# Roots by ln and exp, sums by TensorE, and a split first LayerNorm in a two-layer MetaFormer

## The chip, the core and the metric

The kernel runs on one core of a Trainium2 chip, in float32. The metric is the device time of one execution in microseconds (us). A separately profiled execution gives the trace. The core's engines are TensorE (PE in the profile, its weight loads PEld), VectorE (DVE), ScalarE (ACT), GpSimd (POOL) and SyncE (SP). Each works through its own instructions in order; semaphores tie them together. Data moves by 16 DMA engines, whose transfers are issued from an engine's queue.

## The reference

The input x is (4, 384, 32, 32): four batches, 384 channels, 1024 positions. Two layers, each a mixer and a feed-forward part, with residuals:

```python
# layer 0
x = x + selective_scan_block(layernorm_c(x))
t = tokens(x)
t = t + experts(layernorm(t))
# layer 1
x = x + attention(layernorm_c(x))
t = tokens(x)
out = t + kron_ffn(layernorm(t))
```

The selective scan reads the positions in four directions. For each direction it projects x to 12 + 16 + 16 rows, forms dt by a softplus, and runs `h = h*exp(dt*A) + dt*u*B`, `y = sum_n h*C` over 1024 steps with 16 states per channel. The four directions are added, normalized over channels, scaled, and put through an exact GELU. The feed-forward part of layer 0 chooses two of four experts per token (384 to 1536 to 384, GELU) and adds their outputs weighted by the two gates. Attention has eight heads of 64 with one matrix for queries, keys and values. In the last feed-forward part both matrices are Kronecker products (32 by 12 factors): each token's 384 channels are first multiplied by a vector `c2` of 12 repeated numbers and summed in groups of 12, which leaves 32 numbers per token, called z here.

## The kernel before

The program has two strands. `scan_layer` does layer 0's mixer for batches 0 to 3, one after the other, in 32 units (batch, direction, half of 512 positions). `tail_batch` does everything else of a batch: `route`, `experts`, `combine`, `prologue`, `attention` and `last_layers`. Batch b's tail is woven into the scan of batch b+1 and after; the last batch's routing, experts, attention and last layers stand behind the scan alone, together with what is left of batch 2's. A planner in the framework puts the instructions of both strands in one order per engine; `high_priority` marks those to be put forward (combine, prologue, last layers, and a part of the routing). On the chip the order is fixed.

**The scan.** `start(b)` (L219) loads x of a batch in one transfer and normalizes both halves with `layernorm` (L149). TensorE makes the channel mean by a product with ones (`ln_mean`, L157), DVE subtracts it (L159), ScalarE squares (L166), TensorE sums the squares (`ln_var`, L172), ScalarE takes the root (L178), DVE the reciprocal (L180), TensorE spreads it over the partitions (`ln_rows`, L183) and DVE multiplies (L188). `project` (L289) makes a unit's projections (`xd_ps`, L318), dt by softplus, and writes rows to DRAM, from which they are read back spread over the partitions (`dtr<-dd`, `bcs<-rows`). Chunk by chunk, POOL multiplies dt*u by B (`bx`, L420), ScalarE takes the exponential (`da`, L429), DVE scans (L434), DVE and POOL multiply by C (L441, L448), and TensorE accumulates (`acc`, L455). `finish(b)` (L225) normalizes the sum y, applies Gelu (ScalarE, L228), adds x (POOL, L236) and writes x1 to DRAM. Then the next batch's scan follows.

**ScalarE's tables.** A root needs another activation table than Exp, and Gelu another again. `exp_again` (L141) loads the table with exp and ln back after each root and each Gelu. The instruction is ACT_TABLE_LOAD in the profile: L144 is this reload, and a load on the line of a root is the load for that root.

**The tail.** `route` transposes a batch to tokens, computes gate scores and token statistics, finds for each token its two experts' places, and (L649 to L654, in `spread`) normalizes each block of 128 tokens on DVE and scatters it by POOL's indirect DMA to both places. `experts` runs 11 slots of 256 or 128 rows; weights come by SP. A slot ends with `y_ps` (TensorE, L895), the bias (DVE, L899) and a transfer of y to `made` in DRAM (L900, SP's queue). `combine` (L904) gathers for each token block both experts' rows from `made` (POOL, L913), multiplies each by its gate into PSUM (ScalarE, L920) and adds both to the tokens `xt` (DVE, L924). `prologue` (L930) takes token statistics (`stats`, L516, with a root at L525 and a reciprocal), normalizes (DVE, L531) and transposes to `xc` (`tc_ps`, TensorE, L939). `attention` (L946) begins with products on `xc` (`w_ps`, L964). `last_layers` (L1047) adds the output bias (POOL, L1077), forms the output projection in pairs of token blocks (`o_ps`, L1083, added at L1087), takes the statistics, multiplies all of xt by c2 (`prod`, L1091), sums in groups of 12 (`zt`, L1093), corrects for mean and root (L1098 to L1102), and goes on with `z_ps` (L1108), the hidden products and the output.

**Buffers.** The tail's room has, while the scan runs, 8 buffers `kw` (128x768), 2 of `k12` (128x3072), 5 of `k4` (128x1024), and one pair of PSUM banks that `two` hands out for `w_ps` of combine, `tc_ps`, `s_ps`, `o_ps`, `z_ps` and `h_ps`; for batch 3's attention and last layers there are two such pairs.

Of the kernel before, what the change touches and what calls it, by code (L numbers as in the profile page):

```python
# [12 lines left out]
ALU = mybir.AluOpType  # L13
# [101 lines left out]
class Body:  # L115
    def __init__(self, ctx, tc, a):
        self.tc, self.nc, self.a = tc, tc.nc, a
        nc = self.nc
        const = ctx.enter_context(tc.tile_pool(name="const", bufs=1))
        self.const = const  # L120

        self.cols = const.tile([P, NCOL], F32, tag="cols", name="cols")
        nc.scalar.dma_start(out=self.cols, in_=a["cols"])

        self.ident = const.tile([P, P], F32, tag="ident", name="ident")
        make_identity(nc, self.ident)
        self.ones = const.tile([P, P], F32, tag="ones", name="ones")
        nc.gpsimd.memset(self.ones, 1.0)
        self.eps5 = const.tile([P, 1], F32, tag="eps5", name="eps5")
        nc.gpsimd.memset(self.eps5, 1e-5)  # L130
        self.eps6 = const.tile([P, 1], F32, tag="eps6", name="eps6")
        nc.gpsimd.memset(self.eps6, 1e-6)

        self.minus1 = const.tile([P, 1], F32, tag="minus1", name="minus1")
        nc.gpsimd.memset(self.minus1, -1.0)

        self.c2sum = const.tile([P, 1], F32, tag="c2sum", name="c2sum")
        lo, hi = COL["c2"]
        nc.vector.tensor_reduce(self.c2sum, self.cols[:, lo:hi], AX.X, ALU.add)
# [5 lines left out]

    def col(self, name, i):
        at = COL[name][0] + i
        return self.cols[:, at : at + 1]

    def layernorm(self, src, dst, eps, psum, work):  # L150

        nc = self.nc
        for i in range(NH):
# [16 lines left out]
            for m in range(nm):  # L170
# [6 lines left out]
            self.exp_again(  # L177
                nc.scalar.activation(std, var[:, :nm], AF.Sqrt, bias=eps, scale=1.0 / D).ins  # L178
            )
            nc.vector.reciprocal(std, std)  # L180
# [11 lines left out]
    def scan_layer(self, x1, between):  # L192

        nc, tc, a = self.nc, self.tc, self.a
        with ExitStack() as ctx:
# [23 lines left out]
            def start(b):  # L219
                x = work.tile([P, DC, L], F32, tag="u", name="u")  # L220
                nc.sync.dma_start(out=x, in_=a["x"][b].rearrange("(c p) l -> p c l", p=P))
                self.layernorm(x, x, self.eps6, psum, work)
                return x
# [26 lines left out]
            for _ in self.project(units[0], us[0], wx, work, dram, psum, ahead):  # L250
                pass
            self.under_way = {}
# [232 lines left out]
    def first_layer(self, b, room):  # L485

        self.experts(b, self.slots, room)
        with self.tc.high_priority(offset=FORWARD):
            xt = self.combine(b, *self.place, room)
            return self.prologue(xt, xt, room)  # L490
# [25 lines left out]
    def stats(self, xt, eps, room):  # L516
# [8 lines left out]
        self.exp_again(nc.scalar.activation(rstd, mv[:, :, 1], AF.Sqrt, bias=eps).ins)  # L525
        nc.vector.reciprocal(rstd, rstd)
        return mv[:, :, 0], rstd

    def normalize(self, xt, mean, rstd, out):
        for m in range(MB):  # L530
            self.nc.vector.tensor_scalar(  # L531
                out[:, m, :], xt[:, m, :], mean[:, m : m + 1], rstd[:, m : m + 1],
                op0=ALU.subtract, op1=ALU.mult,
            )
# [71 lines left out]
    def spread(self, b, x1, room):  # L606
# [29 lines left out]
        self.exp_again(nc.scalar.activation(rstd, mv[:, :, 1], AF.Sqrt, bias=self.eps5).ins)  # L636
        nc.vector.reciprocal(rstd, rstd)
        nc.vector.tensor_mul(sc, sc, rstd.unsqueeze(2).to_broadcast([P, MB, NE]))
        nc.vector.tensor_add(sc, sc, self.bg.unsqueeze(1).to_broadcast([P, MB, NE]))
        pos, gate, expert = self.places(sc, room)  # L640
# [4 lines left out]
        for m in range(MB):  # L645
            if m % 2 == 0:
                xt = room.tile([P, 2, D], "k4", "xt")
                nc.sync.dma_start(out=xt, in_=self.tokens(b)[:, m : m + 2, :])
            nc.vector.tensor_scalar(  # L649
                xt[:, m % 2, :], xt[:, m % 2, :], mv[:, m, :1], rstd[:, m : m + 1],  # L650
                op0=ALU.subtract, op1=ALU.mult,
# [155 lines left out]
    def experts(self, b, routed, room):  # L807
# [57 lines left out]
        for s in range(NSLOT):  # L865
# [34 lines left out]
            nc.sync.dma_start(  # L900
# [3 lines left out]
    def combine(self, b, pos, gate, room):  # L904

        nc = self.nc
        xt = room.tile([P, MB, D], "k12", "xt")
        nc.sync.dma_start(out=xt, in_=self.tokens(b))
        got = []
# [7 lines left out]
        for m in range(MB):  # L917
            ps = room.two("w_ps")
            for k in range(TOP):
                nc.scalar.activation(  # L920
                    ps[:, k, :D], got[m][:, k, :], AF.Copy, scale=gate[:, k, m : m + 1]
                )
            for k in range(TOP):
                nc.vector.tensor_add(xt[:, m, :], xt[:, m, :], ps[:, k, :D])  # L924
        nc.sync.dma_start(out=self.tokens(b), in_=xt)
        return xt
# [3 lines left out]
    def prologue(self, xt, xn, room):  # L930

        nc = self.nc
        mean, rstd = self.stats(xt, self.eps6, room)
        self.normalize(xt, mean, rstd, xn)
        xc = room.tile([P, DC, L], "k12", "xc")
        for c in range(DC):
            ps = room.two("tc_ps")
            for m in range(MB):
                nc.tensor.transpose(  # L939
                    ps[:, m // 4, m % 4 * P : (m % 4 + 1) * P], xn[:, m, c * P : (c + 1) * P],  # L940
# [108 lines left out]
    def last_layers(self, b, att, room):  # L1049
# [27 lines left out]
        nc.gpsimd.tensor_add(xt, xt, bout.unsqueeze(1).to_broadcast([P, MB, D]))  # L1077
        for m in range(0, MB, 2):
# [8 lines left out]
            nc.vector.tensor_add(xt[:, m : m + 2, :], xt[:, m : m + 2, :], ps[:, :, :D])  # L1087

        mean, rstd = self.stats(xt, self.eps5, room)
        prod = room.tile([P, MB, D], "k12", "prod")  # L1090
        nc.vector.tensor_mul(prod, xt, c2.unsqueeze(1).to_broadcast([P, MB, D]))  # L1091
        zt = room.tile([P, MB, KR], "zt", "zt")
        nc.vector.tensor_reduce(  # L1093
            zt.rearrange("p m r -> p (m r)"), prod.rearrange("p m (r j) -> p (m r) j", j=KJ),
            AX.X, ALU.add,
        )
# [61 lines left out]
    def second_layer_exact(self):  # L1158

        nc, tc, a = self.nc, self.tc, self.a  # L1160
        with ExitStack() as ctx:
# [10 lines left out]
            for b in range(B):  # L1172
                xc = work.tile([P, DC, L], F32, tag="xc", name="xc", bufs=1)
                att = work.tile([P, HEADS // 2, L], F32, tag="att", name="att", bufs=1)
                with ExitStack() as part:
# [4 lines left out]
                    nc.vector.tensor_copy(xc, self.prologue(xt, xt, room))  # L1180
# [205 lines left out]
```

## Time and profile before

| | |
|---|---|
| median of 3 runs | 4482.44 us (4480.09 to 4482.89) |
| profiled execution | 4517.48 us, span 4513.6 us |
| granted TensorE clock | 0.831 |
| TensorE, VectorE, ScalarE, GpSimd busy | 76, 67, 56, 67% of the span |
| activation table loads | 92 of the exp table again (118.0 us), 28 before a root (35.9 us) |
| experts' products times gates (ScalarE, L920) | 64, 37.3 us |
| adding them (VectorE, L924) | 64, 35.3 us |
| normalizing in the prologue (VectorE, L531) | 32, 23.0 us |
| normalizing in the routing (VectorE, L649) | 32, 30.4 us |
| product with c2 and its sums (VectorE, L1091, L1093) | 4 and 4, 17.3 and 13.3 us |

Each row is a group of instructions of one line and engine: how many there are in the whole execution, and how long they were busy together. The profiled execution takes longer than the timed ones; sums of instruction times are to be held against its own time. In the lines below, `out<-in` names the tiles, sizes are partitions by elements, "xN" counts the instructions; after the bar stand busy time and the mean of one in ns, then the engine's idle time just before them and what ended it. In an ordered listing the first two numbers are start and length in us, and a bracket gives the idle time before it, with its releaser. A line of a stage has its start and end, its length, then the busy time of each engine with the number of instructions, the granted clock, the DMA engines' busy share and GB/s.

### The profile page before, as it was taken

To read this page: it belongs to the slowest core of one execution; us is meant where nothing else is said; L and a number is where in the kernel's file an instruction comes from. 1 tells how busy PE (TensorE), PEld (TensorE's weight loads), DVE (VectorE), ACT (ScalarE), POOL (GpSimd) and SP (SyncE) were. 2 spreads that over 40 slices of the span, in tenths; PEclk is the share of its full clock that TensorE was granted. 3 is DMA by queue.
4 is the path that set the end of the run, shared out by engine and by line. 5 is a ranking of instruction groups with operands and counts; after the bars stand their busy time and mean duration, and the time that the engine had idled before them with its cause. 6 is when DMAs were issued, how large, how long until landed. Compare 5 with 4: busy or idle time off the path is not lost. (4 is left out here: it accounts for less than half of the span.)

```text
span 4513.6 us, 46925 instructions
## 1 busy us (share of the span) xinstructions
PE 3440.6 (76%) x13852; PEld 1652.0 (37%) x13852; DVE 3010.8 (67%) x4344; ACT 2534.3 (56%) x4406; POOL 3037.0 (67%) x1467
## 2 busy tenths in 40 slices
PE   6545554479894787669998588757998689999796
PEld 2111121145552222225555222214555445556333
DVE  4999997878878977977877777896778520002102
ACT  4555554456665676466666577556666444334554
POOL 4999998788987877778988778878889510000100
PEclk7666665589996898669998699858999789999897
DMA  4444554477886533457779443445787543344200
GB/s 119 118 123 118 146 136 106 137 230 209 231 240 181 149 84 104 130 159 226 210 220 275 137 114 101 115 139 170 232 244 232 169 157 115 107 127 153 75 16 15
DMA packets 404361, 684.81 MB, mean 152 GB/s; under 512 B 50944, under 2 KB 206464, under 8 KB 404096
## 3 DMA queue, kind: packets, MB, share of 16 engines
q1 hardware_dynamic: 395360, 656.16, 50.3%
q0 software_dynamic: 8192, 25.17, 1.7%
q8 instruction: 111, 1.82, 0.2%
q14 instruction: 154, 1.26, 0.1%
q10 hardware_dynamic: 544, 0.40, 0.0%
HBM read 561.47 MB, written 120.06 MB: 151 GB/s over the span
## 5 line engine op out<-in xcount | busy, mean ns | idle before, releaser
L420 POOL TENSOR_TENSOR bx<-dtr,bcs 128x1024 f32<-128x1024 f32 x768 | 1797.8, 2366 | 227.7 <-PE acc L455 103.5
L429 ACT ACTIVATE da<-dtr,nega 128x512 f32<-128x512 f32 x1536 | 1045.5, 691 | 1039.4 <-DVE bx L441 569.0
L448 POOL TENSOR_TENSOR bx<-bx,bcs 128x1024 f32<-128x1024 f32 x384 | 903.6, 2358 | 211.8 <-DVE bx L434 88.0
L455 PE MATMUL acc<-bx,sel 128*32 128x512 f32 x3072 | 511.8, 713 | 312.4 <-POOL bx L448 248.8
L879 PE MATMUL h_ps<-xc,w 128*128 128x256 f32 (+1 forms) x3168 | 680.1, 370 | 61.7 <-DVE xc L861 31.5
L895 PE MATMUL y_ps<-w,hs 128*128 128x384 f32 x1824 | 649.9, 509 | 49.8 <-ACT hs L888 44.1
L879 PEld LDWEIGHTS h_ps<-xc,w 128*128 128x128 f32 x3168 | 557.2, 200 | 253.4 <-issue 120.4
L434 DVE TENSOR_TENSOR_SCAN bx<-da,carry,bx 128x512 f32<-128x512 f32 x384 | 474.0, 1269 | 118.6 <-POOL bx L420 65.5
L434 DVE TENSOR_TENSOR_SCAN bx<-da,bx 128x512 f32<-128x512 f32 x384 | 452.2, 1209 | 129.2 <-POOL bx L420 70.3
L434 DVE TENSOR_TENSOR_SCAN da<-da,carry,bx 128x512 f32<-128x512 f32 x384 | 476.5, 1273 | 67.9 <-ACT da L429 62.6
L441 DVE TENSOR_TENSOR bx<-da,bcs 128x512 f32<-128x512 f32 x768 | 509.8, 679 | 3.8
L434 DVE TENSOR_TENSOR_SCAN da<-da,bx 128x512 f32<-128x512 f32 x384 | 456.3, 1218 | 60.7 <-ACT da L429 44.2
L895 PEld LDWEIGHTS y_ps<-w,hs 128*128 128x128 f32 x1824 | 352.3, 198 | 341.7 <-issue 86.4
L992 ACT ACTIVATE ex<-s_ps 128x512 f32<-128x512 f32 x512 | 299.4, 591 | 274.9 <-PE s_ps L987 259.9
L987 PE MATMUL s_ps<-w 64*128 64x512 f32 x1024 | 308.4, 674 | 83.1 <-ACT ex L992 74.2
L1077 POOL TENSOR_TENSOR xt<-xt,wb 128x3072 f32<-128x3072 f32 x4 | 26.8, 6708 | 477.5 <-DMA w<-in_w 345.5
L1036 PE MATMUL o_acc<-ex,vt 128*64 128x512 f32 x1024 | 295.6, 658 | 0.8 <-ACT att L1044 0.8
L455 PEld LDWEIGHTS acc<-bx,sel 128*32 128x32 f32 x3072 | 77.7, 117 | 596.0 <-POOL bx L448 363.8
L884 ACT ACTIVATE hs<-h_ps,bb 128x256 f32<-128x256 f32 (+1 forms) x528 | 194.0, 447 | 128.8 <-PE h_ps L879 128.5
L899 DVE TENSOR_TENSOR y<-y_ps,bb 128x384 f32<-128x384 f32 x76 | 41.6, 548 | 237.6 <-PE y_ps L895 237.6
L913 POOL DMA_INDIRECT got<-made,g_pos x64 | 60.8, 950 | 192.4 <-PE f_acc L1136 159.1
L987 PEld LDWEIGHTS s_ps<-w 64*128 64x128 f32 x1024 | 81.1, 192 | 266.8 <-ACT ex L992 149.1
(216 smaller groups left out, 4021.9 us busy)
## 6 DMA issues: line engine op xcount, KB each, us to landing
w<-in_w SPq DMA_DIRECT2D x352, 576.0 KB
dtr<-dd SPq DMA_DIRECT2D x1536, 128.0 KB
bcs<-rows SPq DMA_DIRECT2D x512, 128.0 KB
dd<-one_e SPq DMA_DIRECT2D x96, 256.0 KB
dd<-mag SPq DMA_DIRECT2D x96, 256.0 KB
rows<-zero SPq DMA_DIRECT2D x76, 192.0 KB
xs<-rows SPq DMA_DIRECT2D x32, 384.0 KB
made<-y SPq DMA_DIRECT2D x32, 384.0 KB
```

The source lines that it names most:

```text
L420: pool = nc.gpsimd.tensor_mul(bx, dtr[q][1], bc[:, 0].unsqueeze(1).to_broadcast([P, 2, HF])).ins
L429: nc.scalar.activation(da, dtr[q][0][:, j, :], AF.Exp, scale=nega[:, col : col + 1])
L434: nc.vector.tensor_tensor_scan(run(h), run(da), run(bx[:, j, :]), 0.0 if first else hold, ALU.mult, ALU.add,)
L441: dve = nc.vector.tensor_mul(bx[:, j, :], h, cg).ins
L448: pool = nc.gpsimd.tensor_mul(bx, bx, cg.unsqueeze(1).to_broadcast([P, 2, HF])).ins
L455: nc.tensor.matmul(acc[lo : lo + DB, :], sel, out[q][:, j, :], start=(g == 0), stop=(g == NG - 1),)
L879: nc.tensor.matmul(ps[:, r, :], w1[(f + r) // wf][:, c, (f + r) % wf * P : ((f + r) % wf + 1) * P], xc[:, c, :], start=(c == 0), stop=(c = ...
L884: nc.scalar.activation(hs[:, f + r, :], ps[:, r, :], AF.Identity, bias=bb[:, f + r : f + r + 1])
L895: nc.tensor.matmul(out[:, :D], hs[:, f, t * P : (t + 1) * P], w2[f // wf][:, f % wf, :], start=(f == 0), stop=(f == FC - 1),)
L987: nc.tensor.matmul(ps[:, o, :], w[rows, j * P : (j + 1) * P], w[rows, halves(i)], start=True, stop=True,)
L992: ins = nc.scalar.activation(ex[:, o, :], ps[:, o, :], AF.Exp, scale=HD**-0.5, accum_out=sums[:, t, 2 * j + o, i : i + 1],).ins
L1036: ins = nc.tensor.matmul(out[cols, :], made[t][1][:, j, cols], ex[:, o, :], start=(j == 0), stop=(j == MB - 1),).ins
```

## The change

1. The table with exp and ln is loaded as ScalarE's first instruction of all.
2. A root's reciprocal is made by two activations of that table, `exp(-0.5 * ln(var + eps))`, in `layernorm` (16 sites), `stats` (8) and the routing (4). The root, both table loads and the reciprocal on DVE go.
3. Normalizing in the routing and in the prologue moves from DVE to ScalarE: Identity with scale = rstd and bias = -mean*rstd, the latter made by one small DVE instruction. The prologue's result goes into the gathered buffers `got`, no longer into `xt`.
4. `combine`: POOL makes, for both experts, eight diagonal 128x128 tiles of the gates; TensorE multiplies them with the gathered rows and adds both experts in PSUM; DVE adds a pair of blocks at once.
5. The last expert slot's `made` transfer is issued from ScalarE's queue instead of SP's.
6. `last_layers`: the product with c2 and its sums are made for each pair of blocks behind its output projection; the product goes to the same PSUM bank.
7. The first batch's x is loaded in two halves. Only its first half is normalized before the first unit's projections, the second half behind them.

```diff
+        nc.scalar.preload_act_table_set("natural_log_exp_and_others")
         self.cols = const.tile([P, NCOL], F32, tag="cols", name="cols")
...
+    def inverse_root(self, out, var, eps, scale=1.0):
+        self.nc.scalar.activation(out, var, AF.Ln, bias=eps, scale=scale)
+        self.nc.scalar.activation(out, out, AF.Exp, scale=-0.5)
...
-    def layernorm(self, src, dst, eps, psum, work):
+    def layernorm(self, src, dst, eps, psum, work, parts=range(NH)):
-        for i in range(NH):
+        for i in parts:
...
-            self.exp_again(
-                nc.scalar.activation(std, var[:, :nm], AF.Sqrt, bias=eps, scale=1.0 / D).ins
-            )
-            nc.vector.reciprocal(std, std)
+            self.inverse_root(std, var[:, :nm], eps, scale=1.0 / D)
...
-                nc.sync.dma_start(out=x, in_=a["x"][b].rearrange("(c p) l -> p c l", p=P))
-                self.layernorm(x, x, self.eps6, psum, work)
+                src = a["x"][b].rearrange("(c p) l -> p c l", p=P)
+                if b > 0:
+                    nc.sync.dma_start(out=x, in_=src)
+                    self.layernorm(x, x, self.eps6, psum, work)
+                    return x
+                for i in range(NH):
+                    nc.sync.dma_start(out=x[:, :, halves(i)], in_=src[:, :, halves(i)])
+                self.layernorm(x, x, self.eps6, psum, work, parts=[0])
                 return x
...
             for _ in self.project(units[0], us[0], wx, work, dram, psum, ahead):
                 pass
+            self.layernorm(us[0], us[0], self.eps6, psum, work, parts=range(1, NH))
...
+    def less_mean(self, mean, rstd, room, tag):
+        less = room.tile([P, MB], tag, "less")
+        self.nc.vector.scalar_tensor_tensor(less, mean, -1.0, rstd, op0=ALU.mult, op1=ALU.mult)
+        return less
...
-            nc.vector.tensor_scalar(
-                xt[:, m % 2, :], xt[:, m % 2, :], mv[:, m, :1], rstd[:, m : m + 1],
-                op0=ALU.subtract, op1=ALU.mult,
+            nc.scalar.activation(
+                xt[:, m % 2, :], xt[:, m % 2, :], AF.Identity,
+                bias=less[:, m : m + 1], scale=rstd[:, m : m + 1],
             )
...
-            nc.sync.dma_start(
+            queue = nc.sync if s + 1 < NSLOT else nc.scalar
+            queue.dma_start(
                 out=made[at : at + size, :].rearrange("(t p) d -> p t d", p=P), in_=y
             )
...
+        diag = []
+        for k in range(TOP):
+            d = room.tile([P, MB, P], "k4", "diag")
+            nc.gpsimd.tensor_mul(
+                d, self.ident.unsqueeze(1).to_broadcast([P, MB, P]),
+                gate[:, k, :].unsqueeze(2).to_broadcast([P, MB, P]),
+            )
+            diag.append(d)
...
-        for m in range(MB):
+        for m in range(0, MB, 2):
             ps = room.two("w_ps")
-            for k in range(TOP):
-                nc.scalar.activation(
-                    ps[:, k, :D], got[m][:, k, :], AF.Copy, scale=gate[:, k, m : m + 1]
-                )
-            for k in range(TOP):
-                nc.vector.tensor_add(xt[:, m, :], xt[:, m, :], ps[:, k, :D])
+            for o in range(2):
+                for k in range(TOP):
+                    nc.tensor.matmul(
+                        ps[:, o, :D], diag[k][:, m + o, :], got[m + o][:, k, :],
+                        start=(k == 0), stop=(k == TOP - 1),
+                    )
+            nc.vector.tensor_add(xt[:, m : m + 2, :], xt[:, m : m + 2, :], ps[:, :, :D])
...
-        return xt
+        return xt, [got[m][:, 0, :] for m in range(MB)]
...
         mean, rstd = self.stats(xt, self.eps6, room)
-        self.normalize(xt, mean, rstd, xn)
+        less = self.less_mean(mean, rstd, room, "less")
+        for m in range(MB):
+            nc.scalar.activation(
+                xn[m], xt[:, m, :], AF.Identity, bias=less[:, m : m + 1], scale=rstd[:, m : m + 1]
+            )
...
-            nc.vector.tensor_add(xt[:, m : m + 2, :], xt[:, m : m + 2, :], ps[:, :, :D])
+            pair = xt[:, m : m + 2, :]
+            nc.vector.tensor_add(pair, pair, ps[:, :, :D])
+            nc.vector.tensor_mul(ps[:, :, :D], pair, c2.unsqueeze(1).to_broadcast([P, 2, D]))
+            for o in range(2):
+                nc.vector.tensor_reduce(
+                    zt[:, m + o, :], ps[:, o, :D].rearrange("p (r j) -> p r j", j=KJ),
+                    AX.X, ALU.add,
+                )
...
-        prod = room.tile([P, MB, D], "k12", "prod")
-        nc.vector.tensor_mul(prod, xt, c2.unsqueeze(1).to_broadcast([P, MB, D]))
-        zt = room.tile([P, MB, KR], "zt", "zt")
-        nc.vector.tensor_reduce(
-            zt.rearrange("p m r -> p (m r)"), prod.rearrange("p m (r j) -> p (m r) j", j=KJ),
-            AX.X, ALU.add,
-        )
```

## The prediction

> **What bounds the kernel now.** I read the table of engine busy times first, then the same busy times by stage, then the routing windows, then the order of time at the start and the end.
>
> The page's first part:
>
> ```profile
> PE 3440.6 (76%) x13852; PEld 1652.0 (37%) x13852; DVE 3010.8 (67%) x4344; ACT 2534.3 (56%) x4406; POOL 3037.0 (67%) x1467
> ```
>
> No engine is full over the span, so the bound moves. By stage (start:end in us, length, then busy time of each engine, granted clock, DMA share, GB/s):
>
> ```profile
> 60.00:790.00 730.00, 389.90 (x1194) 114.81 (x1192) 651.59 (x876) 388.11 (x602) 694.11 (x303) 0.66 0.49 125
> ...
> 2690.00:3554.00 864.00, 710.42 (x2963) 350.55 (x2961) 695.10 (x968) 534.76 (x920) 717.78 (x335) 0.88 0.59 174
> 3554.00:3690.00 136.00, 87.77 (x339) 46.73 (x340) 45.63 (x154) 62.41 (x124) 37.97 (x38) 0.72 0.56 187
> 3690.00:4190.00 500.00, 484.65 (x2011) 284.51 (x2007) 46.87 (x81) 192.13 (x388) 7.66 (x2) 0.98 0.37 117
> ```
>
> The first batch's scan, which has no tail work beside it, is POOL's (694 of 730 us), with DVE close behind. In the scans of batches 1 to 3 POOL and DVE are each busy near 80%: POOL is the steady limit and gives way in stretches. From 3690 us TensorE is the bound (485 of 500). So an edit is worth what it gives POOL or DVE before 3554 us, what it takes from a chain in which both wait, and what it gives TensorE after that. The three routing stretches are DVE's:
>
> ```profile
> 840.00:900.00 60.00, 18.83 (x43) 3.57 (x43) 59.64 (x114) 18.59 (x29) 40.63 (x20) 0.51 0.45 124
> 1860.00:1920.00 60.00, 26.31 (x86) 10.05 (x86) 59.93 (x83) 31.15 (x42) 36.79 (x18) 0.50 0.39 112
> 2940.00:3000.00 60.00, 30.64 (x101) 13.67 (x100) 59.59 (x102) 28.13 (x43) 45.38 (x21) 0.53 0.50 144
> ```
>
> DVE is full for 60 us in each, and POOL has 15 to 23 us to spare.
>
> **What the Trainium skill says.** "ScalarE: Activation LUTs", Table sets: the hidden batching unit: exp and ln share natural_log_exp_and_others, sqrt has another set, so exp, sqrt, exp is two switches. Same page, What ACT_TABLE_LOAD costs: about 1283 ns of load, with a drain of about 1380 ns. The trace has 1283 ns for every load; an activation starts 20 ns after its load, so I count the load alone. "SBUF — State Buffer", Who interferes with whom: DVE and GpSimd share a port pair; two-port DVE forms and DVE operations with two SBUF inputs contend with it, ScalarE and TensorE never do. The trace agrees: the same 128x384 subtract-and-multiply takes 465 ns at its fastest and 2542 ns at its slowest in the first routing stretch. "DMA: Bandwidth & Descriptors", Issuing engines are not separate DMA queues: another issuing engine saves only sequencer time, so the moved `made` DMA is worth no bandwidth.
>
> **The change part by part** (negative is faster).
>
> *Start: −12.* Now the second half's LayerNorm stands before the projections:
>
> ```profile
> 8.08 4.47 PE L157 MATMUL ln_mean<-u,ones 128*128 128x512 f32 x6 [8.08 <-DMA u<-in_x]
> ...
> 19.70 1.28 ACT L178 ACT_TABLE_LOAD   x1 [4.56 <-PE ln_var L172]
> ...
> 34.61 4.80 PE L318 MATMUL xd_ps<-u,wx 128*44 128x512 f32 x6
> ```
>
> The second half's rows are made at 32.61 and xd_ps follows 2.0 us later. The first half's rows are made at 21.62; without the table load (1.28) and the reciprocal they come at about 20.3, so xd_ps at 22.3: −12.3. The halved transfer lands sooner: the whole took 7.3 us, so 0 to 3.5 us. Against it, the second half's LayerNorm (TensorE about 9 us, DVE 4) now stands ahead of the first accumulations; the first POOL multiply waits from 35 to 61 us for projections, softplus and two DMAs, which covers most. I give back 4. The early table load itself is worth nothing: the first Exp waits until 3.79 us for the column DMA, after the load has ended at 2.97. Ends: −8 and −16.
>
> *Table loads in the scan's LayerNorms: −10.* 28 roots lose two loads each: 56 × 1.283 = 72 us of ScalarE, which is not the bound. They count where everybody waits: POOL stands before the final x + y of each batch for the Gelu (72.0 us over four batches), and inside that wait lie two root loads: 4 × 2 × 1.28 = −10. The second activation of each root (0.26) replaces the reciprocal (0.17). Ends: −5, and −20 if the exp loads are in it too.
>
> *Routing's normalization off DVE: −20.* In the three full stretches it takes 11.5, 8.2 and 7.3 us of DVE, together 27.0. ScalarE gets 8 × about 0.6 us in each (between the 476 ns of its 128x384 copy and an estimate of 0.69 from the activation price of that page with two pointers), and is busy 19 to 31 of 60 there. I count three quarters, as scatters on POOL follow. Ends: 0 if POOL's chain takes over at once, −27.
>
> *Combine and prologue in the scan, batches 0 and 1: −10.* Per batch DVE loses 16 × 0.551 + 8 × 0.791 = 15.1 and gains 4 × 0.948 = 3.8; ScalarE loses 16 × 0.584 = 9.3 and gains 8 × 0.6. DVE is the limit about half of the time there: half of 11.3 a batch, rounded down. Ends: 0, −22.
>
> *Diagonal tiles on POOL: +14.* Two 128x1024 products per batch. The trace has no such product; POOL's nearest, the same size with a broadcast operand, takes 2.366 us: 4.7 per batch, on the bound for three batches. The fourth pair runs while POOL is idle. Ends: 0 if made in a POOL wait; +20 if contention lengthens them.
>
> *Combining products on TensorE: +5.* 16 × 0.51 us (an expert's 128x384 product) = 8 per batch, beside waits that exist already in the scan, but they stand as one block that waits for the gathers, with later scan products behind it. Ends: 0, +15.
>
> *Last layers per pair: −5.* In the scan DVE exchanges 4.33 + 3.32 for 4 × 0.95 + 8 × about 0.5 (the reduce row's 1.08 ns per element): equal. The held PSUM bank delays the next pair's products by about 2 us, behind which scan products stand ready. At the end it counts: the whole-tile product and reduce after the last o_ps take
>
> ```profile
> 4439.10 3.34 DVE L1091 TENSOR_TENSOR prod<-xt,wb 128x3072 f32<-128x3072 f32 x1
> ...
> 4442.51 3.32 DVE L1093 TENSOR_REDUCE zt<-prod 128x256 f32<-128x3072 f32 x1
> ```
>
> = 6.66; one pair's share, 0.95 + 2 × 0.5, stays: −4.7. Ends: −3, −6.
>
> *Where the work now stands: 0, from −35 to +50.* The largest unknown. Compared in engine order, the tail's POOL work moves 10 to 20 scan products (24 to 47 us) forward: batch 2's 16 gathers stood after the scan's last product and now stand 10 products before it; its attention starts before the last accumulation. Now, 3554 to 3628 us holds 39.7 us of TensorE work, so up to 34 us of idleness could be filled. But the gathers wait for the last expert's `made`, and the gathers themselves took 20 us, in order ahead of 10 products at 2.37. Batch 3's combine gains from the shorter path (the last y_ps ends at 4184.25, attention's first product starts at 4247.19: 63 us now; about 42 worked out of gathers 21, last pair's product and add, statistics, root, normalizing and transposes), but the 31 us of batch 2's last layers that TensorE does inside that gap now stand ahead of it: −21 + 31 = +10, unless they fill earlier idle time. The last `made` DMA moves to ScalarE's queue, where it waits for y on DVE with scan Exps behind it. I take gain and loss to cancel.
>
> Sum: −12 − 10 − 20 − 10 + 14 + 5 − 5 + 0 = −38. Against the profiled execution (4517.48, span 4513.6 and 3.9 around it): 4479. The median shown, 4482.44, lies 35 us below that execution; the same −38 gives 4444.
>
> **Rivals.**
>
> *Slower: the gathers stand in the scan's way (about 4500).* POOL works in order. Batch 2's last y_ps ended at 3552.9, with the scan's last product, and only 0.6 us after the last y was its DMA issued; the gathers' data came 3 us later. If experts still end there, POOL stands before the gathers while 10 products (24 us) wait behind 20 us of gathers and 5 of diagonals, and batches 0 and 1 pay a smaller wait each: about +55 on −38. It decides from a loss of 38 us. For it: TensorE's experts and the scan now end together. Against: everything in the tail has moved forward together, experts too.
>
> *No relief in the scan (about 4473).* POOL's chain sets all stretches, so DVE's 30 us bring nothing: −12 − 10 − 5 + 14 + 5 = −8 or so. For it: POOL's 694 of 730 us in batch 0. Against: the full DVE stretches.
>
> *The idle stretch is filled (about 4410).* The forecast, with some 34 us of the idleness between 3554 and 3628 gone. For it: the gathers and prologue now precede the scan's end. Against: TensorE must hold ready work then, and batch 3's routing still needs the scan's last LayerNorm.
>
> That the change does not do what it says is excluded only for its early table load.
>
> **How the numbers follow.** Forecast 0.47, filled 0.18, no relief 0.15, slower 0.20. Predicted: 4444, own range 4425 to 4465. The range reaches to 4398 (filled, with the good ends) and to 4498 (the slower case begun, with 1 in 10 above). Within 0.2% (9 us, about what a measurement of this kernel can tell from no change) lies about half of the no-relief case: 0.07. Faster: 0.47 + 0.18 + 0.08 = 0.73; slower 0.20.
>
> **What would show it.** After: 56 fewer table loads; the first POOL multiply near 49 us instead of 61; POOL's waits for the Gelu 2 to 3 us shorter each; DVE no longer full in the routing stretches; the time from the last o_ps to the first z_ps 6 instead of 11 us. Wrong would be: POOL or TensorE standing before batch 2's gathers with scan products behind them, a later last accumulation, or more TensorE idleness between the scan's end and batch 3's attention than now (89 us: the 693 us of three stages less their 604 of work).

## The result, and the profile after

| | median of 5 runs | ratio to before, 95% interval |
|---|---|---|
| before | 4482.44 us (4478.95 to 4487.81) | 1 |
| after | 4452.44 us (4437.41 to 4459.20) | 0.9931 (0.9918 to 0.9945) |

The change makes the kernel 0.69% faster, 31 us by the ratio; the prediction was 38 us (4444). The profiled execution of after took 4452.07 us (span 4450.2), close to the median. That of before had taken 4517.48, most likely because it came from another chip: the experiments below ran in three series, each on a chip of its own, and the kernel before took 4514.25 us in the first, 4510.81 in the second and 4481.68 in the third. The 63 us between the two spans are therefore about half chip and half change. Each ratio is taken within a series; stretches are compared further down between the first two series, in which the kernel before differs by 0.08%.

The page's first part, kernel after:

```profile
PE 3462.1 (78%) x13980; PEld 1644.5 (37%) x13980; DVE 2980.1 (67%) x4252; ACT 2469.7 (55%) x4380; POOL 3050.0 (69%) x1475
```

Busy times move little: TensorE +21, VectorE −31, ScalarE −65, GpSimd +13 us. By stage (columns as before), after:

```profile
47.00:790.00 743.00, 398.97 (x1226) 121.43 (x1225) 655.74 (x878) 380.14 (x602) 694.46 (x303) 0.67 0.45 123
...
3565.00:3696.00 131.00, 114.16 (x501) 45.79 (x499) 27.72 (x108) 69.46 (x177) 22.87 (x22) 0.92 0.43 146
3696.00:4146.00 450.00, 446.42 (x1949) 276.83 (x1945) 45.52 (x86) 185.82 (x336) 10.46 (x3) 1.00 0.41 132
4146.00:4188.00 42.00, 23.12 (x56) 10.56 (x57) 9.23 (x22) 7.42 (x12) 15.21 (x16) 0.75 0.50 155
```

The first batch's scan starts 13 us sooner and has the same 694 us of POOL work in 743 us instead of 730. The scan ends later: its last accumulation at 3568.9 us, before at 3554.0. In the stretch behind it TensorE is far better filled: 114 of 131 us, where it was 88 of 136. The stretch from batch 3's last expert product to its attention is 42 us where it was 63.

The three routing stretches, after:

```profile
840.00:900.00 60.00, 19.11 (x49) 4.11 (x48) 58.23 (x121) 23.68 (x39) 42.76 (x23) 0.58 0.33 97
1840.00:1900.00 60.00, 26.28 (x103) 10.62 (x95) 58.14 (x84) 28.51 (x49) 43.90 (x21) 0.55 0.31 92
2880.00:2940.00 60.00, 33.46 (x117) 13.82 (x115) 59.62 (x106) 28.45 (x50) 45.34 (x21) 0.64 0.36 108
```

VectorE stays full there although its 27 us of normalizing left: other work of it moved up.

The start and the end of after, in order of time:

```profile
17.70 0.26 ACT L150 ACTIVATE ln_std<-ln_var,eps 128x4 f32<-128x4 f32 x1 [4.58 <-PE ln_var L179]
...
47.83 2.36 POOL L432 TENSOR_TENSOR bx<-dtr,bcs 128x1024 f32<-128x1024 f32 x1 [45.65 <-DMA dtr<-dd]
...
4380.38 0.95 DVE L1117 TENSOR_TENSOR xt<-xt,o_ps 128x768 f32<-128x768 f32 x1 [1.21 <-PE o_ps L1112]
4381.36 0.97 DVE L1118 TENSOR_TENSOR o_ps<-xt,wb 128x768 f32<-128x768 f32 x1
...
4383.17 1.01 DVE L1120 TENSOR_REDUCE zt<-o_ps 128x32 f32<-128x384 f32 x2
...
4386.74 1.94 PE L1137 MATMUL z_ps<-ident,z 128*128 128x128 f32 x8 [6.40 <-DVE z L1131]
```

The first POOL product comes at 47.8 us (61.2 before), and z_ps follows the last o_ps by 6.4 us (10.9 before).

### The profile page after: what moved, and what is told of

It reads as the page before. It is cut to its first block, busy times and chain, and to the rows that moved or that the text cites. A ratio compares the mean times of both kernels' runs of the same rounds, so it can differ in the third digit from the quotient of the medians.

```text
span 4450.2 us, 47090 instructions
## 1 busy us (share of the span) xinstructions
PE 3462.1 (78%) x13980; PEld 1644.5 (37%) x13980; DVE 2980.1 (67%) x4252; ACT 2469.7 (55%) x4380; POOL 3050.0 (69%) x1475
## 5 line engine op out<-in xcount | busy, mean ns | idle before, releaser
L889 PE MATMUL h_ps<-xc,w 128*128 128x256 f32 (+1 forms) x3168 | 665.2, 364 | 43.6 <-DVE xc L871 21.1
L889 PEld LDWEIGHTS h_ps<-xc,w 128*128 128x128 f32 x3168 | 547.4, 196 | 228.6 <-issue 92.0
L926 POOL TENSOR_TENSOR diag<-ident,g_picked 128x1024 f32<-128x1024 f32 x8 | 15.0, 1895 | 243.1 <-PE xc_ps L868 223.8
```

The source lines that it names most:

```text
L889: nc.tensor.matmul(ps[:, r, :], w1[(f + r) // wf][:, c, (f + r) % wf * P : ((f + r) % wf + 1) * P], xc[:, c, :], start=(c == 0), stop=(c = ...
```

## Experiments

Two theories stood against each other. **The sum**: each part is worth what its instructions cost or save on the path, as the prediction added them up. **The order**: any edit makes the planner write another order for both strands on all engines, and that order is worth more, either way, than the instructions.

### The kernel before again

No edit.

> The kernel before, profiled a second time, unchanged. Theory A (the first profile was a slow execution): its execution takes about 4482 us, within 10, as the timed runs do, and the trace shows where the first profile's extra 35 us lay. Theory B (profiling this kernel costs 35 us): about 4517 again.

Measured: 4513.71 us for this profiled execution, beside 4514.25 (median) for the timed runs of the same kernel in that series. So neither theory holds: profiling costs nothing, and the series differ, most likely by their chips (nothing here separates the chip from the session). This profile (span 4509.6) serves below as "before" for the first two series.

### One part alone, and the whole without one part

Split and halved load alone (start and the call behind the first projections, as in the change's diff, on the kernel before):

```diff
+                for i in range(NH):
+                    nc.sync.dma_start(out=x[:, :, halves(i)], in_=src[:, :, halves(i)])
+                self.layernorm(x, x, self.eps6, psum, work, parts=[0])
...
+            self.layernorm(us[0], us[0], self.eps6, psum, work, parts=range(1, NH))
```

> Only the first batch's split LayerNorm and halved load on the kernel before. Theory of the sum: the first POOL product comes 12 to 13 us earlier and the end with it, about 4470 us. Rival (order): the written order keeps POOL's products in groups of six and three through the whole first batch instead of 1.5 of its 8 units; a grouped unit takes 2 to 5 us longer than the 83.2 of an alternating one, so batch 0 ends no earlier or later than before (x + y at 802 us or later) and the time is 4482 or above.

Roots by ln and exp with the early load alone:

```diff
-        self.exp_again(nc.scalar.activation(rstd, mv[:, :, 1], AF.Sqrt, bias=eps).ins)
-        nc.vector.reciprocal(rstd, rstd)
+        self.inverse_root(rstd, mv[:, :, 1], eps)
```

> Only the roots by ln and exp and the early table load. Theory of the sum: POOL's waits for the Gelu are 2 to 3 us shorter each, about 4472 us (-10). Rival (loads cost nothing): 4482, within 5.

The whole change without the split:

```diff
-                src = a["x"][b].rearrange("(c p) l -> p c l", p=P)
...
-                for i in range(NH):
-                    nc.sync.dma_start(out=x[:, :, halves(i)], in_=src[:, :, halves(i)])
-                self.layernorm(x, x, self.eps6, psum, work, parts=[0])
+                nc.sync.dma_start(out=x, in_=a["x"][b].rearrange("(c p) l -> p c l", p=P))
+                self.layernorm(x, x, self.eps6, psum, work)
...
-            self.layernorm(us[0], us[0], self.eps6, psum, work, parts=range(1, NH))
```

> The whole change without the split of the first batch. Theory of the sum: 12 us more than the changed kernel, about 4464. Rival (order): the first product comes at about 60 us again, but POOL alternates from the middle of the second unit on, so batch 0 ends within 3 us of 801 as with the split, and the time is that of the changed kernel (4452) or below.

Combining by TensorE alone:

```diff
-                nc.scalar.activation(
-                    ps[:, k, :D], got[m][:, k, :], AF.Copy, scale=gate[:, k, m : m + 1]
-                )
...
+                    nc.tensor.matmul(
+                        ps[:, o, :D], diag[k][:, m + o, :], got[m + o][:, k, :],
+                        start=(k == 0), stop=(k == TOP - 1),
+                    )
```

> Only the combining by TensorE (gate diagonals on POOL, one add per pair of blocks), on the kernel before. Theory of the sum: +14 for the diagonals, +5 for the products, some -5 of relief in the scan, and -10 to -20 on the path from batch 3's last expert product to its attention, which takes 63 us before and about 48 here: between -6 and +9 us. Rival (order): the path is as short, but the scan's end moves by tens of us either way, as with the roots alone.

Normalizing on ScalarE alone, in routing and prologue (the edit in the routing; that in the prologue is as in the change's diff):

```diff
-            nc.vector.tensor_scalar(
-                xt[:, m % 2, :], xt[:, m % 2, :], mv[:, m, :1], rstd[:, m : m + 1],
-                op0=ALU.subtract, op1=ALU.mult,
+            nc.scalar.activation(
+                xt[:, m % 2, :], xt[:, m % 2, :], AF.Identity,
+                bias=less[:, m : m + 1], scale=rstd[:, m : m + 1],
             )
```

> Only the normalizing multiplication on ScalarE instead of VectorE, in the routing and the prologue. Theory of the sum: -25 us (20 from the three full stretches of VectorE, 5 in the prologues), ratio 0.9945. Rival (order): VectorE's work in the routing stretches falls by some 8 us each as summed, but the end of the scan does not follow it; ratio between 0.995 and 1.01.

| kernel | us, and before beside it | ratio, 95% interval | the sum said |
|---|---|---|---|
| split alone | 4553.31, 4514.25 | 1.0093 (1.0074 to 1.0113) | −12 us |
| roots alone | 4541.72, 4514.25 | 1.0057 (1.0042 to 1.0072) | −10 us |
| all but the split | 4494.05, 4514.25 | 0.9954 (0.9939 to 0.9968) | −26 us |
| combining alone | 4518.62, 4510.81 | 1.0017 (1.0009 to 1.0026) | −6 to +9 us |
| normalizing alone | 4486.82, 4510.81 | 0.9946 (0.9933 to 0.9959) | −25 us |

Two of these meet the sum in amount: combining costs 8 us, normalizing brings 24. Beside the second profile of before, their traces tell them apart. With the combining alone the last accumulation comes at 3613 instead of 3557 us, and the rest takes 919 us instead of 953 (in a profiled execution 15 us above its median): the scan's end moved by tens of us, as the rival said, and the agreement is luck. With the normalizing alone POOL is 20 us ahead of before at its 1149th product of 1152, which is near the sum's figure, although VectorE is still busy for 59.4, 59.5 and 58.7 of 60 us in the routing stretches. Batch 2's gathers, which before stood behind the scan, then run ahead of the last two products. So the last accumulation comes only 9 us sooner, and the rest is 16 us shorter.

Two are on the other side of nothing: the split alone loses 42 us and the roots alone lose 26, though the latter take 56 table loads out and add nothing of their size. The whole without the split is at −20 instead of −26: with it the ratio goes from 0.9954 to 0.9931 (0.9943 when measured again), 5 to 10 us where the sum said 12. The intervals of 0.9954 and 0.9943 overlap by most of their width, so this gain is hardly clear of the noise. Its batch 0 ends at 799.5 us, as the rival said, but the time is not the changed kernel's. So the split costs 42 us alone and on top of the other parts brings 10 at most: the parts don't add up.

Where the split's start goes is seen in POOL's products of the first batch, 36 a unit, as starting times in us (from the traces):

| product | before | split alone | after | after, other order |
|---|---|---|---|---|
| 1st | 61.2 | 48.3 | 47.6 | 47.1 |
| 49th | 177.1 | 175.7 | 171.3 | 164.8 |
| 97th | 291.2 | 295.7 | 292.5 | 276.4 |
| 145th | 402.0 | 411.0 | 405.8 | 387.2 |
| batch's x + y ends | 802.1 | 824.7 | 799.2 | 780.7 |

(Before is its first profile; after and its other order are the profiles of the third series.) In an order in which the two kinds of POOL product (times B, times C) alternate, POOL goes from one to the next without a gap, 83.2 us a unit. Where they stand in groups of six and three, it waits at the turns, for VectorE's scans or for TensorE's accumulation: the first four units of after take 95.6, 88.7, 88.4 and 85.4 us, those of before 88.2, 86.3, 83.2 and 83.1. Before, the groups last one and a half units, after three and a half, and with the split alone they last through nearly the whole batch. POOL is the bound here, so its 13 us are gone by the fourth unit.

### The same instructions in another order

Both kernels hold the instructions of their partner (the traces count the same ones, but for two table loads fewer in after's other order). The planner was shown two more table loads behind each root; they are removed once the order is written:

```diff
+        ins = self.nc.scalar.activation(out, out, AF.Exp, scale=-0.5).ins
+        for _ in range(2):
+            with self.tc.issue_after(ins), self.tc.high_priority():
+                ins = self.nc.scalar.preload_act_table_set("natural_log_exp_and_others").ins
+            PHANTOM.add(ins.name)
...
+    for blk in nc.cur_f.blocks:
+        had = blk.instructions
+        left = [x for x in had if x.name not in PHANTOM]
+        if len(left) < len(had):
+            blk.instructions = left
```

> Exactly the instructions of the roots-only kernel, in another order: the planner was shown two more table loads behind each root, which were taken out of the program after it had written the order. Theory of the sum: the same time as roots only (4542 where before takes 4514), within 5 us, since the instructions are the same. Rival (order): it differs from it by over 10 us, to either side; batch 1's gathers now stand at product 827 of POOL's 1152 instead of 835.

> The changed kernel unchanged, on the chip of the other experiments, where the kernel before takes about 4512 us. Expected by every theory: ratio 0.993 (within 0.002), some 4480 us. It is the measure for the kernel with the loads put back (0.9922): loads worth nothing, and the two agree within 0.2%; worth 10 us, and this one is at 0.990.

> Exactly the changed kernel's instructions in another order: the planner was shown two more table loads behind each root, taken out after it had written the order. POOL's products of the first batch alternate from the first unit on instead of from the middle of the fourth. Theory of the sum: the changed kernel's time within 5 us. Rival (order): the first product comes at about 48 us again, and the 13 us are still there at the end of batch 0 (x + y at about 788 instead of 801 us); how the tail then stands (gathers at products 491, 817, 1128 instead of 496, 820, 1142) is worth up to 30 us either way, so a ratio between 0.984 and 0.997, but not 0.993 with batch 0 ending at 801.

| kernel | us, and before beside it | ratio, 95% interval |
|---|---|---|
| roots alone | 4541.72, 4514.25 | 1.0057 (1.0042 to 1.0072) |
| same instructions, other order | 4497.15, 4510.81 | 0.9968 (0.9956 to 0.9979) |
| after again | 4454.96, 4481.68 | 0.9943 (0.9930 to 0.9957) |
| same instructions, other order | 4481.21, 4481.68 | 1.0002 (0.9993 to 1.0011) |

The other order of after lies outside the range that was written for it (0.984 to 0.997), on the slow side. The order alone is worth 0.89% (40 us) for the one set of instructions and 0.59% (26 us) for the other. For after this is shown within one series, since only the order, and what the planner hangs on it, differs; the two orders of the roots ran in different series, each beside its own before. A third pair, under "Carrying the split further", differs by nothing, so an order can be worth this much but need not be. The whole change has been measured at 31 and 26 us; with another order of the same instructions it is worth nothing. The theory of the sum, as a way to forecast the total, falls with this.

After's other order is also instructive in detail. Busy times of 47 to 303 us, first after again, then its other order:

```profile
47.00:303.00 256.00, 146.73 (x419) 42.40 (x418) 220.80 (x308) 130.41 (x207) 232.62 (x101) 0.71 0.42 118
```

```profile
47.00:303.00 256.00, 145.45 (x441) 42.98 (x440) 235.38 (x333) 138.23 (x218) 248.53 (x108) 0.70 0.44 125
```

POOL makes 108 instructions instead of 101 in the same time, and batch 0 ends 18.5 us sooner (780.7). So the start's gain can be kept. But the last accumulation ends at 3579.7 instead of 3564.9, lost above all late in batch 2's scan and early in batch 3's (4 us ahead of after at the 817th product, 28 behind at the 961st; a batch has 288), and from there to the end it takes 900 us instead of 885. In that last part TensorE has 802 us of work instead of 814 and 98 us of idleness instead of 71: batch 3's expert stage alone is 465 us for 448 of work,

```profile
3709.00:4174.00 465.00, 448.05 (x1917) 278.17 (x1913) 44.60 (x82) 182.68 (x325) 10.48 (x3) 0.98 0.40 128
```

where after again has

```profile
3696.00:4145.00 449.00, 445.69 (x1945) 276.63 (x1945) 45.14 (x84) 185.47 (x334) 10.46 (x3) 1.00 0.41 133
```

### The table loads, with the order held

The changed kernel's order is kept and the loads are put back when it is written:

```diff
+    for blk in nc.cur_f.blocks:
+        had, out = blk.instructions, []
+        for x in had:
+            if x.name in own:
+                continue
+            if x.name in ROOTS:
+                out.append(spare.pop())
+            out.append(x)
+            if x.name in ROOTS.values():
+                out.append(spare.pop())
+        if len(out) != len(had):
+            blk.instructions = out
```

> The changed kernel in its own order of instructions, with a table load put back before and after each of its 28 roots (56 loads of the same table, so nothing else moves). Theory of the sum: 10 us slower than the changed kernel (5 to 20), ratio to before about 0.995 against its 0.993. Rival (the loads lie off every path): within 3 us of it. A loss of 30 us or more would say that the loads were worth much more than summed.

Measured: 4477.67 beside 4510.81, ratio 0.9922 (0.9910 to 0.9934), against 0.9943 and 0.9931 for the changed kernel without them. The 56 loads were run (the group of their line):

```profile
L1347 ACT ACT_TABLE_LOAD x56 | 71.8, 1283 | 9.7 <-DVE y L912 8.7
```

72 us more on ScalarE cost no time that these ratios show; the sum's 10 us (0.22%) would have put this kernel at 0.995 to 0.997. Apart from the loads, VectorE, ScalarE, GpSimd and TensorE's products run in the same order in both traces. The rival is right: the loads lie off every path that sets the time.

This kernel has after's order on the chip of the second series, where the kernel before takes nearly the time that it takes in the first, so its trace can be laid beside the second profile of before. Stretches of TensorE, length and idle time in us:

| stretch | before | after's order with loads |
|---|---|---|
| start to the last accumulation | 3557, 950 idle | 3581, 944 idle |
| to the last x + y | 45, 24 idle | 42, 6 idle |
| to batch 3's first expert product | 93, 22 idle | 94, 18 idle |
| to batch 3's last expert product | 483, 15 idle | 451, 3 idle |
| to batch 3's attention | 64, 26 idle | 44, 20 idle |
| to the end | 268, 35 idle | 264, 31 idle |
| total | 4510, 1073 idle | 4476, 1022 idle |

The scan ends 24 us later, and the rest is 58 us shorter. TensorE, with the combining's products on top, is busy 18 us longer and idle 52 us less. Work of batch 2's tail now lies where TensorE stood at the scan's end; that shortens batch 3's expert stage by 32 us, and the path to its attention by 20. The scan pays for it. POOL's last products in order of time, after again:

```profile
3496.28 3.75 POOL L926 TENSOR_TENSOR diag<-ident,g_picked 128x1024 f32<-128x1024 f32 x2
3499.99 4.65 POOL L432 TENSOR_TENSOR bx<-dtr,bcs 128x1024 f32<-128x1024 f32 x2
3504.78 1.01 POOL L935 DMA_INDIRECT got<-made,g_pos  x1
...
3523.61 0.94 POOL L935 DMA_INDIRECT got<-made,g_pos  x1 [0.30 <-issue]
3524.57 2.35 POOL L460 TENSOR_TENSOR bx<-bx,bcs 128x1024 f32<-128x1024 f32 x1
```

Batch 2's two diagonals (3.8 us) and 16 gathers (19.8 us) run ahead of the scan's last products. Before, the gathers stood behind them. The 24 us by which the scan ends later are as large as these two together, and the place agrees: with after's order and the loads, POOL is 1.5 us behind before at the 1142nd of its 1152 products and 21.5 behind at the 1143rd, which follows the gathers. POOL does not wait for the gathers' data.

### Carrying the split further

In the changed kernel POOL waits before the last chunks of the scans of batches 1 and 2, because the next batch's input LayerNorm stands before their accumulations on TensorE (order of time, after again):

```profile
1599.05 6.99 POOL L432 TENSOR_TENSOR bx<-dtr,bcs 128x1024 f32<-128x1024 f32 x3 [24.05 <-PE acc L467]
```

So the halved load and split were given to all batches, once in the planner's order, once in the order that it writes with the added loads:

```diff
-                if b > 0:
-                    nc.sync.dma_start(out=x, in_=src)
-                    self.layernorm(x, x, self.eps6, psum, work)
-                    return x
...
-            self.layernorm(us[0], us[0], self.eps6, psum, work, parts=range(1, NH))
...
+                    if units[n + 1][1:] == (0, 1):
+                        self.layernorm(us[nb], us[nb], self.eps6, psum, work, parts=range(1, NH))
```

> The changed kernel with the halved load and the split LayerNorm in all four batches instead of the first alone. Theory: in the changed kernel POOL stands 24 and 21 us before the last chunks of the scans of batches 1 and 2, since the next batch's input LayerNorm, both halves, stands before their accumulations on TensorE; with half of it there the two waits fall to about 12 us each, 20 to 25 us faster than the changed kernel, ratio about 0.988. Rival (order): the waits fall as said, but the tail is moved too (gathers at 479, 805, 1127), and the end does not follow: 0.993 or above.

> The same instructions as with the split in all batches, with the order that the planner writes when it is shown two more table loads behind each root (taken out afterwards): POOL alternates from the first unit on. Theory: batch 0 ends at about 788 us and the two waits at the batch ends are halved: 30 to 40 us faster than the changed kernel, ratio 0.985. Rival: no better than the changed kernel, 0.993, because TensorE's work after the scan takes the gain back as waiting.

Measured: 4494.78 and 4494.87 beside 4481.68, ratios 1.0030 (1.0018 to 1.0042) and 1.0031 (1.0019 to 1.0043): slower than the changed kernel and a little slower than before. The wait at 1599 is gone, but POOL waits at and behind the batch's end (order of time, split in all batches):

```profile
1727.58 6.71 POOL L1101 TENSOR_TENSOR xt<-xt,wb 128x3072 f32<-128x3072 f32 x1 [13.65 <-DMA wb<-in_wb]
...
1753.12 6.97 POOL L428 TENSOR_TENSOR bx<-dtr,bcs 128x1024 f32<-128x1024 f32 x3 [11.46 <-PE acc L463]
...
2723.36 11.60 POOL L428 TENSOR_TENSOR bx<-dtr,bcs 128x1024 f32<-128x1024 f32 x5 [14.76 <-PE acc L463]
```

Against after again, POOL makes up 25 us where the wait went (from 32 us behind at the 540th product to 7 at the 555th) and loses them again round the batch's end (37 behind at the 600th). In the other order batch 0 ends at 769.0 us, 30 sooner than in after, and the scan still ends 33 us later than there. (That is the last x + y, 3643.1 against 3610.4.) The first rival is right. The second is right that nothing is gained, but not in its reason: the time is lost in the scan, and behind the last accumulation the kernel takes 891 us, where after again takes 885. Here the same instructions in two orders take the same time. No kernel here is clearly faster than the changed one.

## Why the prediction was right, and where it was not

The direction, the range and nearly the amount were right (−38 told, −31 and −26 measured), but the amount is luck in good part. The forecast put −33 us into the stretch up to the scan's end and −5 behind it. The table of stretches above has +24, 20 of it the gathers that now run ahead of the scan's last products, and −58. A later last accumulation was one of the prediction's own signs of being wrong, and it came in (3569 instead of 3554 us). Terms that carried the sum failed, and the term that was put at zero with 85 us between its ends decides the result.

- **Start, −12.** The instructions do what was said: xd_ps at 21.2 us (told: 22.3, less what the halved load brings), first POOL product 13.4 us sooner. The failed step is "I give back 4": all 13 came back within four units, and 4 more. The 4 that were meant are there: in the first unit POOL waits 4.1 us for an accumulation, where it did not wait before. About 10 us go to the grouped order of POOL's products, which holds for three and a half units instead of one and a half. The other order keeps the gain in batch 0 and loses it later.
- **Table loads, −10.** Wrong: 0, with the order held. The step that failed is that a load inside POOL's wait for the Gelu counts in full. Those waits did not shrink by 10 us but grew from 72.0 to 98.3 over the batches, and with the loads put back they are not longer than without (95.5 and, in after again, 99.1). The last, beside attention work of batch 2, went from 16.9 to 38.7 (before, then after):

```profile
3592.87 7.37 POOL L236 TENSOR_TENSOR x<-x,y 128x512 f32<-128x512 f32 x6 [16.87 <-ACT y L228]
```

```profile
3602.63 4.93 POOL L247 TENSOR_TENSOR x<-x,y 128x512 f32<-128x512 f32 x4 [38.69 <-ACT y L239]
```

- **Normalizing off VectorE, −20 and part of −10.** The part alone brought 24 us. But the stated sign of it, VectorE no longer full in the routing stretches, did not come in after (58.2, 58.1 and 59.6 of 60), nor with the part alone. So the amount agrees while the reason is not shown, and with after's order (and the loads) it does not arrive: POOL is not ahead of before at its 1142nd product. A cost was left out: the small instruction that makes −mean*rstd. In the prologues of batches 0 to 2 it takes 12.7, 11.6 and 10.8 us, with ScalarE's normalizing behind it; in batch 3's, where POOL has ended its products, 0.17. The group of its line, and order of time in after:

```profile
L543 DVE SCALAR_TENSOR_TENSOR less<-mv,rstd 128x8 f32<-128x8 f32 x8 | 35.9, 4485 | 1.8 <-ACT rstd L151 1.8
```

```profile
1426.00 12.68 DVE L543 SCALAR_TENSOR_TENSOR less<-mv,rstd 128x8 f32<-128x8 f32 x1 [0.61 <-ACT rstd L151]
...
1431.73 6.92 POOL L432 TENSOR_TENSOR bx<-dtr,bcs 128x1024 f32<-128x1024 f32 x3
1438.60 2.44 DVE L446 TENSOR_TENSOR_SCAN bx<-da,carry,bx 128x512 f32<-128x512 f32 x2
```

  It ends with POOL's run of products (1431.73 + 6.92 = 1438.65). The Trainium skill's page "SBUF — State Buffer", Who interferes with whom, says that a VectorE instruction with two SBUF inputs contends with GpSimd instructions that read SBUF; the trace agrees. The prediction cited that and applied it only to what the change removes. In batch 0 the shorter combine is eaten up, in part at least by this: from its last expert product to its attention it takes 62 us before and 64 after. In batch 1 it takes 95 and 64, but the split alone, which has no other combine, has 67 there: that is the order.
- **Diagonals, +14.** They take 1.895 us on average instead of 2.366: 3 × 2 × 1.9 = 11.
- **Combining on TensorE, +5.** Mis-sized at its root: the row's 0.51 us is for one record, and each product has two. After has 128 records of 0.594 us for its 64 products, 60.5 us of TensorE and not 33. Much of it falls in waits: the part alone cost 8 us where all of its terms together had said −6 to +9.

```profile
L943 PE MATMUL w_ps<-got,diag 128*128 128x384 f32 x128 | 60.5, 594 | 43.5 <-DMA got<-made,g_pos 31.9 <-DVE xt L947 11.6
```

- **Last layers, −5.** Right: 10.9 became 6.4 us, in every run that has this part, in whatever order.
- **Where the work stands, 0 from −35 to +50.** The path from batch 3's last expert product to its attention, worked out at 42 us, is 42, and 42 to 44 in every run that has the combining. But the prediction credited its 21 us to the combining, and the split alone, which does not have it, takes 45. What these runs share is that batch 2's last layers no longer lie in the path, as the prediction said. So most of the 21 us is the order. Those layers did find earlier idle time: batch 3's expert stage is 32 us shorter, part of the 58 gained behind the scan, of which the scan's end gives back 24. Its ends were right to be wide: the same instructions gave 40, 26 and 0 us more or less.
- **Rivals.** Two of them came in part, and together. Of the slower one, the 20 us of gathers and the diagonals ahead of the scan's last products are there (19.8 + 3.8 us); the rest of its 55, POOL standing before the gathers for their data, is not, so it stayed under the 38 us from which it would have decided. Of the filled idle stretch, 18 of 34 us came between the last accumulation and the last x + y (idle 24, then 6), and more behind it.

## What to carry to other kernels

Where a planner writes the order, an edit is priced twice: once by its instructions, and once by the new order of everything else. In three pairs of the same instructions that was worth 40, 26 and 0 us of some 4480, and no term of the sum was above 20. Before a gain of that size is put down to an edit, run the same instructions in another order, or hold the order and put the removed work back. An amount that agrees is not enough: look whether the time was won in the stretch where the sum put it. And ask of every small instruction that is added, not only of large ones that are removed, which engine it contends with while it runs.

## What the hardware showed that was not expected

- A 128x8 VectorE instruction took between 0.15 and 12.7 us. The three long ones ended when POOL's unbroken run of 128x1024 products ended. What gets it out of that, such as one operand in PSUM, was not tried.
- 56 table loads (71.8 us of ScalarE) cost nothing with the order held, and the same program took 4482 us in the series on one chip and 4511 and 4514 in those on two others, 0.7% more.
- What stays open: which feature of an order makes it good. Neither the place of the gathers in POOL's order nor the time at which batch 0 ends tells it (780.7 and 769.0 us went with slower kernels). How after's stretches would lie beside before's on one chip was not measured, and the moved `made` transfer and the last layers per pair were not run alone.
